# Layer 0's self-attention: the second head's weights turned by VectorE in blocks of 32 and moved by DMA; stacks built with fewer DMA issues

## The chip, the cores and the metric

The kernel runs on one core of a Trainium2 chip. The core has a matrix engine (TensorE, PE), a vector engine (VectorE, DVE), an activation engine (ScalarE, ACT), a general engine (GpSimd, POOL) and a queue engine that mostly issues DMAs (SyncE, SP). Tiles live in SBUF, 128 partitions wide; matmul results land in PSUM, in banks of 128 x 512 float32. The metric is the device time of one launch in microseconds; runs of one kernel are given with their median.

## The reference

A decoder with two layers, six sublayers in all, each with a residual and a layer normalisation behind it. The batch is 2, the sequence 1024, the width 256, in float32. Of the six, the change is in the first:

```python
def _L0_attn_ref(x, w_q, w_k, w_v, w_o):        # 16 heads, d_k 64
    scale = 1.0 / sqrt(64)
    q = einsum('bsd,hdk->bhsk', x, w_q)         # k and v the same with w_k, w_v
    scores = einsum('bhqk,bhmk->bhqm', q, k) * scale
    weights = softmax(scores, axis=-1)
    z = einsum('bhqm,bhmk->bhqk', weights, v)
    z = z.transpose(0, 2, 1, 3).reshape(b, s, h * dk) @ w_o
    return x + z

x = layernorm(x + L0_attn(x))
x = layernorm(x + L0_xattn(x, ctx))             # cross-attention and a small MLP
x = layernorm(x + L0_ffn(x))                    # 8 experts, entmax gates
x = layernorm(x + L1_attn(x))                   # 16 heads of 16
x = layernorm(x + L1_xattn(x, ctx, mask))
x = layernorm(x + L1_ffn(x))                    # quantised
```

So the first sublayer's result is 2x + z, normalised. The gates of the expert layer are an entmax: a power of a half (a square root) is taken once in them.

## The kernel before

`l0_attn` (from L205) works on head pairs: two heads of one batch entry, 16 pairs `u` in all. A pair has eight steps of 128 queries each, so the main loop has 128 steps `n`. Every step handles both heads of its pair, `h` = 0 and 1.

The stages of one pair are these.

- `load(u)` (L225) fetches the pair's `w_q`, `w_k` and `w_v` with six DMAs of 64 KB into a tile of the pool `wqkv`, which has two buffers. It runs 12 steps before the pair's first step.
- `project(u, k, blk)` makes q and k of both heads, 64 rows each, transposed, 512 columns at a time. ACT copies the result out of PSUM into half of a tile of the pool `x`. It runs 9 steps ahead for k and 5 steps ahead for q.
- `split` cuts each of these blocks in two parts that float32r matmuls can multiply well: DVE masks off the low bits (L262, `top`), and POOL subtracts that from the whole (L263, in place, on 128 x 512). Then SP copies the parts into stacks (L278). In the q stack of a head, `top` lies over the rest; the k stacks of a head hold `top` twice and the rest twice. One matmul over 128 rows then adds two of the partial products. A pair needs 16 of these DMAs for k and 8 for q, 128 KB each.
- `values` makes v for the pair, as two halves, 7 and 3 steps ahead.
- `scores(n)` (L311; L304 for the first pair, which isn't split) puts 128 queries against 1024 keys into a `wide` tile of two PSUM banks. There are two such tiles, one for each head.
- `most` (L325, DVE) takes each row's negated maximum, `exponentials` (L330, ACT) the exponential of 128 x 1024 with its row sum, and `normalised` the reciprocal of the sum (L338, DVE) and the multiplication with it (L339, POOL).
- `turn` (L352) transposes the head's 128 x 1024 weights on PE, as eight blocks of 128 x 128 into two banks, and `copy` takes each bank into a tile of the pool `weights` (L70 on DVE, L74 on ACT), one bank each.
- `mix` (L373), every second step, multiplies the turned weights of two steps (256 queries) with v: 16 matmuls, eight for each head.
- `output` (L390, L396, L398) multiplies the gathered heads with `w_o`, after each four pairs, in the odd steps, and adds 2x.

The order of PE, DVE and ACT is written out by hand in the main loop. Step `n` computes the scores and exponentials of step `n + 2` and turns the weights of step `n`:

```python
for n in range(steps):
    scores(n + 2)
    most(n + 2, 0)
    ps = turn(n, 0)
    copy(n, 0, 0, ps, nc.scalar)
    exponentials(n + 2, 0)
    copy(n, 0, 1, ps, nc.vector)
    most(n + 2, 1)
    exponentials(n + 2, 1)
    normalised(n + 2, 0)
    if n % 2 == 0:
        mix(n // 2 - 1)
    else:
        others(n - 1)
        others(n)
    ps = turn(n, 1)
    normalised(n + 2, 1)
    copy(n, 1, 0, ps, nc.vector)
    copy(n, 1, 1, ps, nc.scalar)
    parted(n)
```

`others` holds the loads, projections, values and output projections; they run in the odd steps. `parted` holds the calls of `split`. What POOL and SP do is put in order by the scheduler, within what the data allows.

Three further places are touched. `constants` (L107) loads small inputs during the first steps of the stage. In the expert layer, `entmax` (L715 to L773) is a generator, `gates`, whose six pieces are run as jobs inside the second and third round (`n` = 1 and 2) of the loop that computes the experts; its third `yield` comes right after the power, on POOL (L759), and the next piece begins with DVE's use of it (L761). `prepare` (L1308) makes things ready for the second layer. The pools that matter: `weights` has 5 buffers of 128 x 2048, `x` 6 and `r` 4 of 128 x 1024, `p` (the exponentials) 5 of 128 x 1024.

Of the kernel before, what the change touches and what calls it, by code (L numbers as in the profile page):

```python
# [14 lines left out]
ALU = mybir.AluOpType  # L15
# [17 lines left out]
class Decoder:  # L33
# [73 lines left out]
    def constants(self):  # L107

        nc, t, const = self.nc, self.t, self.const
        rows = const.tile([P, P], F32, name="rows")  # L110
# [18 lines left out]
        self.lbv = row("lbv", t["L1_attn_b_qkv"][2 * D : 3 * D], D)  # L129
        self.lbp = row("lbp", t["L1_attn_b_proj"], D)  # L130
# [6 lines left out]
        ctxn = const.tile([P, D], F32, name="ctxn")  # L137
# [71 lines left out]
    def l0_attn(self):  # L209
# [5 lines left out]
        with ExitStack() as s:  # L215
            pool = lambda n, k: s.enter_context(self.pool(n, k))
            pwp, qkp, vp, pp = pool("wqkv", 2), pool("qk", 2), pool("v", 2), pool("p", 5)
# [20 lines left out]
            def project(u, k, blk):  # L238
                ps = self.bank()
                for c in range(2):  # L240
                    nc.tensor.matmul(
                        ps, lhsT=wqkv[u][:, k, c, :], rhs=xT[2 * (u // NP) + blk][:, c, :],
                        start=c == 0, stop=c == 1,
                    )
                if u == 0:
                    if k == 0:
                        out = qs[0, blk] = qkp.tile([P, 512], F32R, tag="q0", name="q0", bufs=3).bitcast(F32)
                    else:
                        if blk == 0:
                            ks[0] = qkp.tile([P, S], F32R, tag="k00", name="k00").bitcast(F32)  # L250
                        out = ks[0][:, blk * 512 : (blk + 1) * 512]
                    self.evac(out, ps, None if k else 0.125, by=nc.scalar)
                    return
                both = self.xp.tile([P, 4, D], F32, tag="x", name="xg").rearrange(
                    "p (a i) d -> p a (i d)", a=2
                )
                halves[u, k, blk] = both[:, 0, :], both[:, 1, :]
                self.evac(both[:, 0, :], ps, None if k else 0.125, by=nc.scalar)

            def split(u, k, blk):  # L260
                x, top = halves.pop((u, k, blk))
                nc.vector.tensor_scalar(top.bitcast(I32), x.bitcast(I32), -4096, None, ALU.bitwise_and)  # L262
                nc.gpsimd.tensor_tensor(x, x, top, ALU.subtract)  # L263
                cols = slice(blk * 512, (blk + 1) * 512)
                for h in range(2):
                    rows = slice(64 * h, 64 * h + 64)
                    if k == 0:
                        st = qs[u, h, blk] = qkp.tile([P, 512], F32R, tag=f"q{h}", name=f"q{h}", bufs=3)
                        stacks = [(st, (top, x))]
                    else:  # L270
                        if blk == 0:
                            ks[u, h] = [
                                qkp.tile([P, S], F32R, tag=f"k{h}{i}", name=f"k{h}{i}") for i in range(2)
                            ]
                        stacks = [(ks[u, h][i][:, cols], (part, part)) for i, part in enumerate((top, x))]
                    for st, parts in stacks:
                        for i, part in enumerate(parts):
                            nc.sync.dma_start(st[64 * i : 64 * i + 64, :].bitcast(F32), part[rows, :])  # L278
# [15 lines left out]
            def scores(n):  # L294
# [20 lines left out]
                for h in range(2):  # L315
                    prob[n, h] = (
                        sc[h], self.sm.tile([P, 1], F32, tag="nm", name="nm"),
                        self.sm.tile([P, 1], F32, tag="sum", name="sum"),
                        pp.tile([P, S], F32, tag="p", name="p"),
                    )  # L320
# [20 lines left out]
            turned = {}  # L341
# [22 lines left out]
            def mix(m):  # L364
# [5 lines left out]
                for kt in range(8):  # L370
                    for h in range(2):
                        rows = slice(64 * h, 64 * h + 64)
                        nc.tensor.matmul(  # L373
                            av[rows, 0:256], lhsT=vals[u][:, kt, rows], rhs=turned[m, h][:, kt, :],
                            start=kt == 0, stop=kt == 7,
                        )
# [46 lines left out]
            for u in range(B * NP):  # L423
                first = 8 * u
                at(first - 12, load, u)
# [23 lines left out]
            with self.tc.manual_schedule(engines=engines):  # L449
# [14 lines left out]
                begin(1)  # L464
                parted(-1)
                wo = self.weight(t["L0_attn_w_o"].rearrange("(g p) d -> p g d", p=P), NP, D)
                next(constants)
                for n in range(steps):
                    scores(n + 2)
                    most(n + 2, 0)  # L470
                    ps = turn(n, 0)
                    copy(n, 0, 0, ps, nc.scalar)
                    exponentials(n + 2, 0)
                    copy(n, 0, 1, ps, nc.vector)
                    most(n + 2, 1)
                    exponentials(n + 2, 1)
# [6 lines left out]
                    ps = turn(n, 1)  # L483
                    normalised(n + 2, 1)
                    copy(n, 1, 0, ps, nc.vector)
                    copy(n, 1, 1, ps, nc.scalar)
# [319 lines left out]
    def l0_ffn(self):  # L806
        nc, t = self.nc, self.t
        HT = GT // 2
        with ExitStack() as s:
# [157 lines left out]
            with self.tc.manual_schedule(engines=engines):  # L967
                start = [begin(b) for b in range(B)]
                mixed = None
                for n in range(len(steps) + 1):  # L970
# [6 lines left out]
                    if n in (1, 2):  # L977
                        for k in range(3):
                            jobs[4 + 4 * k] = lambda: next(gates)
# [328 lines left out]
    def prepare(self, tmp):  # L1308
        nc, t, late = self.nc, self.t, self.late
        H = 16  # L1310
        mask = tmp.tile([P, T // P, SK], U8, name="mask")
# [442 lines left out]
```

## Time and profile before

| what | us |
|---|---|
| three runs | 2685.15, 2685.04, 2682.86 (median 2685.04) |
| the profiled execution, its own time | 2682.37 |
| its span | 2680.6 |
| of the span, up to 930: layer 0's self-attention | 930 |
| 930 to 1190: cross-attention, and the expert layer's start | 260 |
| 1190 to 1230: the gates' last pieces, beside the experts | 40 |
| 1230 to 1900: the experts, then the second layer's projections and attention | 670 |
| 1900 to the end: the rest of the second layer | 781 |

The busy time of the engines in these stretches, as the stretch table gives it, with the granted clock of PE:

| stretch | PE | DVE | ACT | POOL | PE clock |
|---|---|---|---|---|---|
| 30 to 930 | 893.50 | 561.92 | 473.74 | 368.27 | 1.00 |
| 930 to 1190 | 242.84 | 92.98 | 59.64 | 56.14 | 0.93 |
| 1190 to 1230 | 33.84 | 21.43 | 8.45 | 20.44 | 0.87 |
| 1230 to 1900 | 667.62 | 363.48 | 218.18 | 231.91 | 1.00 |
| 1900 to 2680 | 701.91 | 594.00 | 381.45 | 118.11 | 0.93 |

How to read the lines that follow. A group of instructions is given as line, engine, operation, output from inputs, shapes and count, then its busy time in us and the mean of one instruction in ns, then how long the engine stood idle just before them and what ended most of that. A line of the timeline is: start in us, duration, engine, line, operation, output from inputs, shapes and count, and in brackets the wait before it with its releaser. A line of the stretch table is: the stretch, its length, then for each engine its busy time and count of instructions, then the granted clock of PE, the busy share of the DMA engines and GB/s. "SPq" is SP's queue, where a duration is the time that issuing took.

### The profile page before, as it was taken

What the parts mean: (1) busy time and instruction counts of PE and PEld (TensorE: products, weight loads), DVE (VectorE), ACT (ScalarE), POOL (GpSimd) and SP (SyncE); (2) the same over time, 40 slices, a digit from 0 to 9 for tenths busy, and PEclk for the clock granted to TensorE, in tenths of its full rate; (3) what the DMA queues carried; (4) which work ended last, traced back from release to release, by engine and by line L of the source; (5) the groups of instructions that cost most, each with busy time, mean ns of one, the idle gap of its engine ahead of it and who ended that gap; (6) DMA issues with size and microseconds to landing.
All of it is one profiled execution on the core that took longest, in us unless ns stands there. A gap on an engine that the chain in (4) does not pass through costs nothing. (4 is left out here: it accounts for less than half of the span.)

```text
span 2680.6 us, 41386 instructions
## 1 busy us (share of the span) xinstructions
PE 2562.0 (96%) x16113; PEld 1910.0 (71%) x16113; DVE 1641.2 (61%) x3204; ACT 1151.9 (43%) x1808; POOL 798.1 (30%) x615
## 2 busy tenths in 40 slices
PE   8999999999999999899999999999979999998975
PEld 5777777777777656688999999999954444444652
DVE  4666566666656532245555565554667978895686
ACT  4555455545545522122333333333315655664344
POOL 3344344334444321242333333342311000100421
PEclk9999999999999999998999999999988999999996
DMA  4223223222322020100010010010030321110000
GB/s 123 60 56 83 54 54 70 60 54 64 76 54 50 15 75 16 34 5 17 24 32 17 27 33 32 12 44 5 1 61 3 59 37 32 32 33 1 1 1 32
DMA packets 87906, 102.95 MB, mean 38 GB/s; under 512 B 39496, under 2 KB 57504, under 8 KB 87712
## 3 DMA queue, kind: packets, MB, share of 16 engines
q1 hardware_dynamic: 87200, 99.27, 16.2%
q8 instruction: 128, 2.10, 0.3%
q10 hardware_dynamic: 512, 1.05, 0.2%
q14 instruction: 66, 0.54, 0.1%
HBM read 34.21 MB, written 2.10 MB: 14 GB/s over the span
## 5 line engine op out<-in xcount | busy, mean ns | idle before, releaser
L339 POOL TENSOR_SCALAR p<-p,rs 128x1024 f32<-128x1024 f32 x256 | 287.1, 1122 | 524.2 <-DVE rs L338 524.1
L1126 DVE TENSOR_REDUCE most<-bank 128x1 f32<-128x512 f32 x512 | 325.9, 685 | 55.2 <-PE bank L1120 47.1
L325 DVE TENSOR_REDUCE nm<-wide 128x1 f32<-128x1024 f32 x256 | 311.8, 1219 | 65.2 <-PE wide L311 44.6
L330 ACT ACTIVATE p<-wide,nm 128x1024 f32<-128x1024 f32 x256 | 286.1, 1118 | 96.3 <-DVE rs L338 85.2
L1169 ACT ACTIVATE w<-wide 128x1024 f32<-128x1024 f32 x256 | 248.3, 1022 | 138.1 <-PE wide L1163 129.4
L74 ACT COPY w<-bank 128x512 f32<-128x512 f32 x260 | 152.2, 586 | 321.6 <-PE bank L352 317.2
L352 PEld LDWEIGHTS bank<-ident,p 128*128 128x128 f32 x2048 | 232.6, 141 | 66.8 <-POOL p L339 25.0
L352 PE MATMUL bank<-ident,p 128*128 128x128 f32 x2048 | 270.8, 275 | 3.7 <-ACT w L74 2.2
L311 PE MATMUL wide<-k,q 128*128 128x512 f32 x960 | 252.4, 404 | 3.4 <-ACT p L330 3.4
L70 DVE COPY w<-bank 128x512 f32<-128x512 f32 x260 | 179.1, 689 | 107.7 <-PE bank L352 98.9
L373 PE MATMUL acc<-w,v 128*64 128x256 f32 x2048 | 237.8, 384 | 0.1
L874 ACT ACTIVATE mhT<-mhT,cols 128x256 f32<-128x256 f32 (+1 forms) x256 | 143.2, 607 | 149.9 <-DVE mhT L902 98.9
L373 PEld LDWEIGHTS acc<-w,v 128*64 128x64 f32 x2048 | 143.1, 137 | 76.5 <-issue 12.7
L311 PEld LDWEIGHTS wide<-k,q 128*128 128x128 f32 x960 | 171.2, 189 | 36.5 <-ACT p L330 5.4
L885 PE MATMUL unit<-xT,w 128*128 128x256 f32 x768 | 183.5, 381 | 0.0
L785 POOL TENSOR_TENSOR hs<-hs,mhT 128x1024 f32<-128x1024 f32 x31 | 103.4, 3336 | 262.0 <-DVE hs L783 262.0
L942 DVE SCALAR_TENSOR_TENSOR r<-acc,gates,r 128x128 f32<-128x128 f32 x256 | 77.8, 346 | 140.5 <-PE acc L933 140.5
L1120 PE MATMUL bank<-kst,qst 64*128 64x512 f32 x512 | 149.6, 483 | 12.4 <-DVE most L1126 12.1
L1120 PEld LDWEIGHTS bank<-kst,qst 64*128 64x128 f32 x512 | 70.3, 193 | 121.4 <-DVE most L1126 95.2
L885 PEld LDWEIGHTS unit<-xT,w 128*128 128x128 f32 x768 | 141.3, 191 | 17.2 <-issue 0.7
L181 POOL TENSOR_TENSOR rstd<-ve,nhalf 128x4 f32<-128x4 f32 (+2 forms) x28 | 26.1, 932 | 391.6 <-DVE ve L179 391.2
L1183 PE MATMUL acc<-w,v 128*32 128x512 f32 x1024 | 137.0, 607 | 0.0
(321 smaller groups left out, 4412.1 us busy)
## 6 DMA issues: line engine op xcount, KB each, us to landing
k<-xg SPq DMA_DIRECT2D x240, 128.0 KB, 2.4
w<-in_L_ffn_W SPq DMA_DIRECT2D x16, 1024.0 KB, 5.3
q<-xg SPq DMA_DIRECT2D x120, 128.0 KB, 2.3
qst<-qh SPq DMA_DIRECT2D x60, 64.0 KB, 2.4
qst<-ql SPq DMA_DIRECT2D x60, 64.0 KB, 2.4
kst<-kh SPq DMA_DIRECT2D x60, 64.0 KB, 2.9
kst<-kl SPq DMA_DIRECT2D x60, 64.0 KB, 2.4
xg<-in_x SPq DMA_DIRECT2D x4, 512.0 KB, 4.4
```

Source lines behind the costliest of these rows:

```text
L70: nc.vector.tensor_copy(out, in_)
L74: nc.scalar.copy(out, in_)
L311: nc.tensor.matmul(sc[h][:, kb, :], lhsT=qs[u, h, qt // 4][:, at : at + P], rhs=ks[u, h][i][:, kb * 512 : (kb + 1) * 512], start=i == 0, s ...
L325: nc.vector.tensor_reduce(nm, sc, AX.XY, ALU.max, negate=True)
L330: nc.scalar.activation(p, sc.rearrange("p a c -> p (a c)"), AF.Exp, bias=nm, accum_out=sum_)
L339: nc.gpsimd.tensor_scalar(p, p, rs, 1.0, ALU.mult, ALU.mult)
L352: nc.tensor.transpose(ps[:, k * P : (k + 1) * P], p[:, kt * P : (kt + 1) * P], self.ident)
L373: nc.tensor.matmul(av[rows, 0:256], lhsT=vals[u][:, kt, rows], rhs=turned[m, h][:, kt, :], start=kt == 0, stop=kt == 7,)
L885: nc.tensor.matmul(v[:, m, :], lhsT=up[e][k][:, f : f + P], rhs=self.halves[g][k], start=k in (1, 2, 5) and m == 0, stop=True, skip_group_ ...
L1120: nc.tensor.matmul(sc[a], lhsT=stack[b, jp, "q"][rows, q0 : q0 + P], rhs=stack[b, jp, "k"][rows, kb * 512 : (kb + 1) * 512], start=True, s ...
L1126: nc.vector.tensor_reduce(most[n][:, kb, qt, h : h + 1], sc[a], AX.X, ALU.max, negate=True)
L1169: nc.scalar.activation(slot[:, k, :], ps[k].rearrange("p a q -> p (a q)"), AF.Exp, scale=0.25)
```

## The change

It has five parts.

1. *The second head's weights* are no longer transposed on PE. DVE transposes each 32 x 32 block of the 128 x 1024 tile within its partition quarter (`turn_blocks`), into a tile of a new pool `blocks` that holds two steps. Every second step `move_blocks` brings the blocks into the places that a full transposition gives them: 16 copies of 32 partitions x (8 runs of 64 elements), of which 4 stay in their quarter and are made by POOL, and 12 go to another quarter by DMA, 4 issued by ACT and 8 by SP, 64 KB each. The turned tile has its queries in another order, and `mix` writes the second head's output through a permuted view that puts them back.
2. *The order of a step* changes: DVE's block transposition of step `n + 1` stands between the maxima of the two heads, ACT's moves stand between the exponentials, and the first head's two copies swap their engines. The second head's exponentials now lie in tiles of the pool `r`, and `p` has 3 buffers.
3. *The stacks.* POOL's subtraction is written straight into the stacks, once for each head (64 x 512, eight for each pair in place of four of 128 x 512). `top` of both k blocks lies side by side in one tile, so that the k stacks take four DMAs of 256 KB from `top` and two of 256 KB for the rest, from the half that was written to the other; the q stacks take four of 128 KB.
4. *The weights' buffers:* `wqkv` has one buffer, and `load` runs 11 steps ahead.
5. *Around it:* two of the constants' tiles move into a tile of `r`, two biases of the second layer are loaded in `prepare`, and the six pieces of `gates` run as four jobs of the second round, at the places 4, 7, 10 and 13, and two of the third, at 8 and 12, in place of three each at 4, 8 and 12.

```diff
-            pwp, qkp, vp, pp = pool("wqkv", 2), pool("qk", 2), pool("v", 2), pool("p", 5)
+            pwp, qkp, vp, pp = pool("wqkv", 1), pool("qk", 2), pool("v", 2), pool("p", 3)
+            bp = pool("blocks", 2)
...
             def split(u, k, blk):
-                x, top = halves.pop((u, k, blk))
+                cols = slice(blk * 512, (blk + 1) * 512)
+                x, top = (a[:, cols] for a in halves[u, k])
                 nc.vector.tensor_scalar(top.bitcast(I32), x.bitcast(I32), -4096, None, ALU.bitwise_and)
-                nc.gpsimd.tensor_tensor(x, x, top, ALU.subtract)
...
+                own = [slice(64 * h, 64 * h + 64) for h in range(2)]
+                for h, rows in enumerate(own):
                     if k == 0:
                         st = qs[u, h, blk] = qkp.tile([P, 512], F32R, tag=f"q{h}", name=f"q{h}", bufs=3)
-                        stacks = [(st, (top, x))]
+                        nc.gpsimd.tensor_tensor(st[rows, :], x[rows, :], top[rows, :], ALU.subtract)
+                        nc.sync.dma_start(st[own[1 - h], :].bitcast(F32), top[rows, :])
...
-                    for st, parts in stacks:
-                        for i, part in enumerate(parts):
-                            nc.sync.dma_start(st[64 * i : 64 * i + 64, :].bitcast(F32), part[rows, :])
+                        nc.gpsimd.tensor_tensor(ks[u, h][1][rows, cols], x[rows, :], top[rows, :], ALU.subtract)
+                if k and blk:
+                    for h, rows in enumerate(own):
+                        for half in own:
+                            nc.sync.dma_start(ks[u, h][0][half, :].bitcast(F32), halves[u, k][1][rows, :])
+                    for h, rows in enumerate(own):
+                        st = ks[u, h][1].bitcast(F32)
+                        nc.sync.dma_start(st[own[1 - h], :], st[rows, :])
...
+            def turn_blocks(n):
+                if not 0 <= n < steps:
+                    return
+                m, qt = divmod(n, 2)
+                p = prob.pop((n, 1))[-1]
+                if qt == 0:
+                    blocks[m] = bp.tile([P, 32, 2, 32], F32, tag="blocks", name="blocks")
+                nc.vector.transpose(blocks[m][:, :, qt, :], p.rearrange("p (j q) -> p j q", q=32))
+
+            def move_blocks(n):
+                m, qt = divmod(n, 2)
+                if qt == 0 or not 0 <= n < steps:
+                    return
+                to = turned[m, 1] = self.weight(None, 8, 256)
+                src = blocks.pop(m).rearrange("p (k r) t q -> p k r (t q)", r=4)
+                dst = to.rearrange("p k (i q) -> p k i q", i=4)
+                for d in range(4):
+                    for i in range(4):
+                        r = (i + d) % 4
+                        a, b = src[32 * i : 32 * i + 32, :, r, :], dst[32 * r : 32 * r + 32, :, i, :]
+                        if d == 0:
+                            nc.gpsimd.tensor_copy(b, a)
+                        else:
+                            (nc.scalar if d == 1 else nc.sync).dma_start(b, a)
...
+                        out, p = av[rows, 0:256], turned[m, h][:, kt, :]
+                        if h:
+                            out = out.rearrange("p (t i q) -> p i t q", t=2, i=4)
+                            p = p.rearrange("p (i t q) -> p i t q", t=2, i=4)
...
-                at(first - 12, load, u)
+                at(first - (11 if u else 12), load, u)
...
                 for n in range(steps):
                     scores(n + 2)
                     most(n + 2, 0)
+                    turn_blocks(n + 1)
+                    exponentials(n + 2, 0)
+                    move_blocks(n + 1)
                     ps = turn(n, 0)
-                    copy(n, 0, 0, ps, nc.scalar)
-                    exponentials(n + 2, 0)
-                    copy(n, 0, 1, ps, nc.vector)
+                    copy(n, 0, 0, ps, nc.vector)
                     most(n + 2, 1)
+                    copy(n, 0, 1, ps, nc.scalar)
                     exponentials(n + 2, 1)
                     normalised(n + 2, 0)
                     if n % 2 == 0:
...
-                    ps = turn(n, 1)
                     normalised(n + 2, 1)
-                    copy(n, 1, 0, ps, nc.vector)
-                    copy(n, 1, 1, ps, nc.scalar)
                     parted(n)
...
-                    if n in (1, 2):
-                        for k in range(3):
-                            jobs[4 + 4 * k] = lambda: next(gates)
+                    for k in {1: (4, 7, 10, 13), 2: (8, 12)}.get(n, ()):
+                        jobs[k] = lambda: next(gates)
```

## The prediction

> **What bounds the kernel now.** I read first the page's span and engine table, then the stretch table for one head pair, then the timeline of two steps, then what each queue waited for. A group below means one head pair: eight steps of 128 queries.
>
> ```profile
> span 2680.6 us, 41386 instructions
> PE 2562.0 (96%) x16113; PEld 1910.0 (71%) x16113; DVE 1641.2 (61%) x3204; ACT 1151.9 (43%) x1808; POOL 798.1 (30%) x615
> ```
>
> ```profile
> core 0: us, PE busy (x) PEld busy (x) DVE busy (x) ACT busy (x) POOL busy (x), PEclk, DMA share, GB/s
> 400.00:454.40 54.40, 54.40 (x369) 40.89 (x368) 34.67 (x59) 30.07 (x53) 23.18 (x20) 1.00 0.31 66
> ```
>
> That stretch is one group: weight loads for two successive pairs are issued 54.4 us apart, at 414.47 and 468.85. TensorE (PE) is busy throughout at full clock and every other engine has room. In start-to-start times a group is four steps with `mix` (scores 1.94, first turn 0.96, mix 3.60, second turn 0.86: 7.36), two with projections (1.93, 0.87, 3.43, 0.86: 7.1) and two with values (5.4), 54.4 in all. The two heads turn 16 blocks a step, so half of that is what the change can free.
>
> What would take over is seen where PE has little to do, at the end of the stage:
>
> ```profile
> 893.07 1.20 PE L311 MATMUL wide<-k,q 128*128 128x512 f32 x4 [0.45 <-ACT p L330]
> 893.70 1.11 ACT L330 ACTIVATE p<-wide,nm 128x1024 f32<-128x1024 f32 x1 [0.69 <-DVE rs L338]
> 894.71 0.19 ACT L330 ACTIVATION_READ_ACCUMULATOR p<-wide,nm 128x1 f32 x1
> 895.01 0.17 DVE L338 RECIPROCAL rs<-sum 128x1 f32<-128x1 f32 x1 [1.35 <-POOL p L339]
> 895.09 0.67 DVE L70 COPY w<-bank 128x512 f32<-128x512 f32 x1
> 895.26 1.12 POOL L339 TENSOR_SCALAR p<-p,rs 128x1024 f32<-128x1024 f32 x1 [0.33 <-DVE rs L338]
> 895.67 1.22 DVE L325 TENSOR_REDUCE nm<-wide 128x1 f32<-128x1024 f32 x1
> ```
>
> PE waits here for an exponential. There is a ring: second head's exponential, its reciprocal 1.31 later (895.01 after 893.70), normalisation on POOL, the next maxima, the next exponential. Now it is hidden, because PE takes longer.
>
> **The change, part by part.** *PE:* eight transposes leave each step, 0.86 start to start: 8 x 0.86 = 6.9 a group, 54.4 to 47.5. The permuted output of the second head's mix has runs of 32 elements; at 0, since mix keeps its instruction count, and if each slowed by a tenth it would cost 0.18 a step with mix.
>
> *DVE:* a copy of 0.69 leaves each step and one 32x32-block transpose of 128x1024 enters. No row has it. Below it lies the two-elements-a-cycle row (L262, 444 ns for 512, so at most 0.9), above it two passes at the reduction's rate, 2.4. It is nearest to the reduction of the same 1024 elements at 1.22, 1.14 to the next instruction as rows overlap. DVE goes from 34.7 to about 34.7 - 5.5 + 9.8 = 39, still below PE. What matters is its place: it stands between the two maxima, in order, and waits for POOL's normalisation of the step before.
>
> *The ring, from the start of a second head's exponential:* reciprocal at 1.31, normalisation at 1.56 to 2.68, transpose from 2.78 (the first maximum, 1.22 from 1.39, fits beside it), next instruction 1.14 later at 3.92, copy 0.58, second maximum 1.22, and 0.11 to its exponential (895.67 + 1.22 to the next in such steps): 5.83 a step. That is close to the 47.5 / 8 = 5.94 that PE needs, so the small things decide.
>
> *ACT:* a copy of 0.59 leaves each step; four DMA issues enter every second step, between the two exponentials. The nearest issue has as many pieces of 256 B (64 KB):
>
> ```profile
> 414.47 0.89 SPq L225 DMA_DIRECT2D wqkv<-in_L_attn_w_q  x2
> 415.40 0.97 SPq L225 DMA_DIRECT2D wqkv<-in_L_attn_w_k  x2
> 430.35 10.50 SPq L278 DMA_DIRECT2D k<-xg  x16
> ```
>
> 0.93 for two is 0.47 each (0.37, as the weights of the expert layer, to 0.65, as the stacks, 10.5/16). They can start when the transpose is done, 3.92; 4 x 0.47 brings 5.8, the copy queued behind them 0.49, and the exponential starts at 6.4 in place of 5.83. Behind ACT stands DVE's reciprocal, and behind it POOL. A step with mix is then 6.4, which PE needs too (1.94 + 0.87 + 3.60). A group: 4 x 6.4 + 2 x 6.25 (projection, PE) + 2 x 5.85 = 49.8, and the masking of the top bits (0.38 each, two of them, in front of a maximum in two steps, partly beside a wait) makes it 51.
>
> *POOL* is where I expect the gain to go. Its order, as the scheduler leaves it, is: four subtractions after a projection, four block copies, then the two normalisations of the step.
>
> ```profile
> L339 POOL TENSOR_SCALAR p<-p,rs 128x1024 f32<-128x1024 f32 x256 | 287.1, 1122 | 524.2 <-DVE rs L338 524.1
> L263 POOL TENSOR_TENSOR xg<-xg 128x512 f32<-128x512 f32 x60 | 78.4, 1325 | 29.5 <-DVE xg L262 29.5
> L1036 POOL MEMSET w<- 32x128 f32 x4 | 0.8, 197 | 0.2
> L1041 POOL MEMSET cz<- 128x512 f32 x1 | 0.5, 529 | 0.1
> L1034 POOL MEMSET w<- 128x128 f32 x2 | 0.4, 206 | 14.4 <-PE unit L885 14.4
> ```
>
> The subtractions become twice as many, each on 64 partitions. The memsets on 32 and on 128 partitions take 197 and 206 ns, so fewer partitions save nothing: 1.30 each (0.65, were it halved, to 1.33). A block copy has 512 elements a partition: between the memset's 0.53 and half a normalisation plus its fixed part, 0.66; I take 0.6 (0.3 if partitions did count, 1.33 if it ran as a two-input operation). Between two normalisations of a second head POOL then has 4 x 1.30 + 4 x 0.6 + 2 x 1.12 = 9.8 in a step that lasts 6.4 + 0.75 = 7.15. The transpose of the next step waits 2.7, and behind it on DVE the copy, the second maximum, and so ACT, the scores and PE. Twice a group, of which some half microsecond in all is caught up again: 51 + 5 = 56, 1.6 above now; over 15 groups +24.
>
> *Stretches with output projections* cost 13.8 now in each of three batches (groups of 57.8 and 64.6). Half of these matmuls fall into the odd steps in which PE would now wait: -7 each, -21. The stage: +3.
>
> *SP and DMA:* 24 stack issues a group become 10 larger ones, 32 moves join. A move has two steps, some 12.5 us, to land before its mix. After a projection, SP first waits for the subtractions (5.2), then sends eight moves, 8 x 0.47 = 3.8, with landing 2.4 as the stacks: 11.4 plus the last stacks, 1-2, inside the 15 that remain to that mix (two steps, scores and a turn). Cover is thin; without it PE would wait 1 to 3 once a group. At 0. The other loads are 12 us ahead of use.
>
> *Start:* one weight buffer in place of two. The second pair's loads wait for the first's values (PE, 21.5), four issues 1.9 and landing 2.1 bring 25.5, where that projection now starts at 21.54: +4. Nothing hides it.
>
> *Expert layer:* the power on POOL moves a job earlier and gets its time.
>
> ```profile
> 1196.21 10.54 POOL L759 TENSOR_TENSOR esq<-u,eroot 128x64 f32<-128x64 f32 x1 [1.89 <-DVE u L758]
> 1206.79 0.23 DVE L761 TENSOR_TENSOR esq<-emean,esq 128x64 f32<-128x64 f32 x1 [10.14 <-POOL esq L759]
> ```
>
> PE stood still for 5.95 behind this, then ran 6.7 us at half clock, 3 more: -9 (0 if DVE meets another wait). The moved biases and constants ride on SP ahead of use: 0.
>
> *Clock.* PE would now stand still 2 to 3 us twice a group, and the trace has a price for that:
>
> ```profile
> 26.50:29.90 3.40, 0.85 (x5) 0.29 (x2) 2.52 (x3) 1.55 (x3) 0.06 (x1) 1.00 0.01 1
> 929.90:933.30 3.40, 1.29 (x11) 0.84 (x8) 2.05 (x5) 2.72 (x6) 1.20 (x2) 0.99 0.02 5
> 933.30:936.70 3.40, 3.31 (x16) 2.04 (x18) 1.11 (x2) 0.52 (x2) 1.04 (x1) 0.51 0.00 0
> ```
>
> A wait of 2.5 near 27 kept the clock, one of 2.2 near 931 halved it for 3.4 us, a loss of 1.7, and it would fall on the steps with mix, where PE has nothing to spare. 30 waits x 1.7 = 51 at worst, 0 at best; with one in two, +25.
>
> The page "TensorE: Matmul & The Clock Gate" of the Trainium skill (Part 1: The HAM clock gate) asks for an idle window of about 3.4 us before the clock halves. By that rule waits of 2.7 would cost nothing and the sum would be 25 lower; the row near 931 speaks against it. The skill's "SBUF — State Buffer" (SBUF: two separate sides) lets GpSimd be shut out by DVE only when DVE runs two-port or has two SBUF inputs; were a transpose to count as that, POOL would lose up to 8 x 1.2 a group more, by the rule nothing, and no run shows it yet.
>
> **Sum**, against the profiled execution, 2682.4 (span 2680.6, 1.8 around it): +3 + 4 - 9 + 25 = +23, 2705. The median of the runs, 2685.0, lies 2.7 above that execution: 2708.
>
> **Rivals.** (1) *POOL is in time, so faster.* If subtraction and copy together take under (7.15 - 2.24)/4 = 1.23 in place of 1.9, the transpose never waits. The group is 51, -3.4 x 15 = -51, some 7 a batch of output projections still fits into PE's gaps, -15 with the thin end of it, then +4 and -9, no clock loss: 2614. For it: POOL is idle 58% of a group; against it: the memset rows. If the ring gave nothing at all, PE's 47.5 would set -104, 2576. (2) *The transpose runs two passes* (2.3): the ring grows 1.14 in every step, of which 6.8 a group shows: +105 beside the 5 of POOL, 2790. For it only that no row has it. (3) *A block copy costs 1.1 and more*, as a two-input operation would: 4 x 0.5 twice a group and then in every second step: about +110, 2800. (4) *Moves land late*: PE waits at mix once a group, 15 x 2 = +30, 2740; DMA share 0.31 with room speaks against it.
>
> **How the numbers follow.** Forecast 0.55, rival (1) 0.25, (2) and (3) 0.08 each, (4) 0.04. The forecast's own range is 2683 (no clock loss) to 2735 (all). The range for eight in ten goes down into (1), to 2640, and up to 2785, short of (2). About 0.2%, 5.4 us, is what a measurement here tells from no change: faster 0.32 (all of (1) and a lower end of the forecast), same 0.13, slower 0.55.
>
> **What would show it.** In the profile after: groups of about 56 with PE busy under 90% in them; DVE's transposes near 1.2 and, twice a group, waiting 2 to 3 on POOL's normalisation; block copies 0.5 to 0.7, subtractions near 1.3; ACT's issues about 0.5; the granted clock under 1.00 in the stage; DVE's wait on the power gone. I am wrong if the transposes find POOL done, if PE stays near 100% there, or if mix waits on a DMA.

## The result and the profile after

The changed kernel takes 2757.81 us (median of four runs, 2754.06 to 2764.29), the kernel before 2683.95 beside it: a ratio of 1.0277, 95% interval 1.026 to 1.0295. It is slower, as forecast, but by 74 us where 23 were forecast.

The page of the changed kernel, its span and engine table:

```profile
span 2762.5 us, 39964 instructions
PE 2522.1 (91%) x15086; PEld 1838.2 (67%) x15089; DVE 1712.4 (62%) x3204; ACT 1081.8 (39%) x1680; POOL 1031.3 (37%) x931
```

PE is busy 40 us less, and yet the span is 82 longer. One pair in the stretch table (the wqkv issues that were 54.4 apart are now 59.8 apart, 398.97 and 458.80):

```profile
400.00:460.00 60.00, 50.41 (x304) 35.45 (x304) 39.70 (x58) 25.68 (x45) 38.09 (x40) 0.97 0.47 95
```

PE now stands still for 9.6 of 60 us, and no other engine is near 60. So the bound is a chain across engines, not one engine's work.

To see which chain, I took the start of the second head's exponential in every step, from the timeline of ACT, and its distances. This is worked out from the trace, for one ordinary pair of each kernel, in order of the pair's steps (in the second distance the projection of k ran, in the sixth that of q, in the fourth and eighth the values):

```
                    distances between the second heads' exponentials, us              sum
before   at 420.0   7.35  7.09  7.36  5.38  7.36  7.10  7.35  5.39                    54.4
after    at 409.6   5.71 10.63  5.83  7.42  5.71  8.74  7.72  7.36                    59.1
after, last pair, no projections: 7.20 and 6.4-6.5 in turn                            54.6 for eight
```

Before, the steps are PE's. After, there is a short step of 5.71, the ring as forecast (5.83), and a step of 7.2 to 10.6, in which ACT issues its four moves. Even without any projection the two together are 13.65, as long as before's 54.4 / 4 = 13.6, projections included (before's last pair, without projections, has 7.35 + 5.30 = 12.65). The timeline of the engines in the step of 10.63:

```profile
416.81 1.12 POOL L349 TENSOR_SCALAR r<-r,rs 128x1024 f32<-128x1024 f32 x1 [0.31 <-DVE rs L348]
417.03 1.51 DVE L265 TENSOR_SCALAR xg<-xg 128x512 int32<-128x512 int32 x2 [0.31 <-ACT xg L74]
418.30 5.44 POOL L278 TENSOR_TENSOR k<-xg 64x512 fp32r<-64x512 f32 x4 [0.36 <-DVE xg L265]
420.86 4.41 ACTq L379 DMA_DIRECT2D w<-blocks  x4
422.47 0.13 DVE L348 RECIPROCAL rs<-sum 128x1 f32<-128x1 f32 x1
423.80 2.57 POOL L377 COPY w<-blocks 32x512 f32<-32x512 f32 x4
425.46 0.59 ACT L74 COPY w<-bank 128x512 f32<-128x512 f32 x1 [4.49 <-issue]
425.95 1.12 ACT L340 ACTIVATE r<-wide,nm 128x1024 f32<-128x1024 f32 x1
426.47 1.12 POOL L349 TENSOR_SCALAR p<-p,rs 128x1024 f32<-128x1024 f32 x1
427.19 0.16 DVE L348 RECIPROCAL rs<-sum 128x1 f32<-128x1 f32 x1 [3.99 <-ACT r L340]
427.21 1.19 PE L318 MATMUL wide<-k,q 128*128 128x512 f32 x4 [3.38 <-ACT r L340]
427.56 1.13 POOL L349 TENSOR_SCALAR r<-r,rs 128x1024 f32<-128x1024 f32 x1
```

ACT is in its four issues ("ACTq", which the engine table doesn't count as busy) from 420.86 to 425.3. The copy behind them waited 4.49, the exponential comes at 425.95, DVE's reciprocal and PE's scores wait for that. POOL's burst, four subtractions and four copies, lies beside the issues and ends at 426.4, just in time. Ahead of all this DVE's two masks (L265) take 1.51, and the first maximum (418.47) and the transposition (419.60) stand behind them. The costs of the parts, from the page's groups:

```profile
L363 DVE STREAM_TRANSPOSE blocks<-r 128x1024 f32<-128x1024 f32 x128 | 158.6, 1239 | 30.8 <-POOL r L349 25.0
L377 POOL COPY w<-blocks 32x512 f32<-32x512 f32 x256 | 155.5, 608 | 64.8 <-DVE blocks L363 45.6
```

The subtractions, from the group table of the stage alone, and ACT's issues, from the table of one source line (least, median and greatest duration of one in ns, first and last start):

```profile
L271 POOL TENSOR_TENSOR q<-xg 64x512 fp32r<-64x512 f32 x60 | 78.3, 1305 | 11.5 <-DVE xg L265 8.1
```

```profile
L379 ACTq DMA_DIRECT2D w<-blocks x256: 592/626/1752, 41.3 to 1031.0; - x128
```

Transposition, block copy and subtraction cost what the forecast took (1.24, 0.61, 1.31). The issue does not: 0.626 in place of 0.47, and up to 1.75.

Of the 82 us between the two profiled executions (the changed kernel's is the slowest of its four, 6.5 above their median), 93.2 arise in the stage of the change (its last exponential starts at 1024.85 in place of 931.66), and 11 are won behind it. Within the stage the first eight steps cost 20.2 more (78.8 for 58.6), the last pair 2.2, the fourteen pairs between 70.2 (879.3 for 809.1), 5.0 each; the first exponential is 0.6 later.

### The profile page after: what moved, and what is told of

Same layout as the page of the kernel before. It is cut to its first block, busy times and chain, and to the rows that moved or that the text cites. A ratio compares the mean times of both kernels' runs of the same rounds, so it can differ in the third digit from the quotient of the medians.

```text
span 2762.5 us, 39964 instructions
## 1 busy us (share of the span) xinstructions
PE 2522.1 (91%) x15086; PEld 1838.2 (67%) x15089; DVE 1712.4 (62%) x3204; ACT 1081.8 (39%) x1680; POOL 1031.3 (37%) x931
## 5 line engine op out<-in xcount | busy, mean ns | idle before, releaser
L318 PE MATMUL wide<-k,q 128*128 128x512 f32 x960 | 296.8, 443 | 116.3 <-ACT r L340 86.0
L340 ACT ACTIVATE p<-wide,nm 128x1024 f32<-128x1024 f32 x128 | 142.7, 1115 | 250.3 <-DVE nm L335 196.3
L415 PE MATMUL acc<-w,v 128*64 128x256 f32 x2048 | 236.5, 382 | 0.0
L349 POOL TENSOR_SCALAR p<-p,rs 128x1024 f32<-128x1024 f32 x128 | 143.7, 1123 | 246.3 <-DVE rs L348 240.1
L415 PEld LDWEIGHTS acc<-w,v 128*64 128x64 f32 x2048 | 142.3, 137 | 75.8 <-issue 12.5
L377 POOL COPY w<-blocks 32x512 f32<-32x512 f32 x256 | 155.5, 608 | 64.8 <-DVE blocks L363 45.6
L340 ACT ACTIVATE r<-wide,nm 128x1024 f32<-128x1024 f32 x128 | 143.1, 1118 | 92.5 <-DVE rs L348 92.5
L363 DVE STREAM_TRANSPOSE blocks<-r 128x1024 f32<-128x1024 f32 x128 | 158.6, 1239 | 30.8 <-POOL r L349 25.0
L349 POOL TENSOR_SCALAR r<-r,rs 128x1024 f32<-128x1024 f32 x128 | 143.9, 1125 | 84.4 <-DVE rs L348 84.2
L74 ACT COPY w<-bank 128x512 f32<-128x512 f32 x132 | 76.8, 583 | 228.5 <-DMA w<-blocks 83.3
L390 PEld LDWEIGHTS bank<-ident,p 128*128 128x128 f32 x1024 | 138.0, 157 | 28.6 <-issue 8.8
L390 PE MATMUL bank<-ident,p 128*128 128x128 f32 x1024 | 153.5, 300 | 1.8 <-DVE w L70 1.8
```

Of the source, the lines that this page charges most:

```text
L318: nc.tensor.matmul(sc[h][:, kb, :], lhsT=qs[u, h, qt // 4][:, at : at + P], rhs=ks[u, h][i][:, kb * 512 : (kb + 1) * 512], start=i == 0, s ...
L340: nc.scalar.activation(p, sc.rearrange("p a c -> p (a c)"), AF.Exp, bias=nm, accum_out=sum_)
L349: nc.gpsimd.tensor_scalar(p, p, rs, 1.0, ALU.mult, ALU.mult)
L363: nc.vector.transpose(blocks[m][:, :, qt, :], p.rearrange("p (j q) -> p j q", q=32))
L377: nc.gpsimd.tensor_copy(b, a)
L390: nc.tensor.transpose(ps[:, k * P : (k + 1) * P], p[:, kt * P : (kt + 1) * P], self.ident)
```

## The experiments

The theory at first: ACT's issues in the ring set the loss. The rivals: POOL's burst behind the projections, as forecast; moves that land late; the one weight buffer at the start. All times below are medians; the kernel before ran at 2683.05 to 2684.84 beside them, and the changed kernel at 2757.8. Its own runs lie 10 us apart, so a gain of 6 to 10 from one edit is hardly told from none.

### One limit removed at a time

*All moves on SP.*

```diff
-                            (nc.scalar if d == 1 else nc.sync).dma_start(b, a)
+                            nc.sync.dma_start(b, a)
```

> The changed kernel with all twelve moves of two steps issued by SP; ACT issues none. In the changed kernel's trace ACT's four issues take 2.6 us in plain steps and 4.4 in the step behind the k projection, between the two exponentials. Theory A (ACT's issues alone set the loss): the plain steps with mix go from 7.2 to 5.8-6.4 and the step behind the k projection from 10.7 to about 7.3; a pair falls from 60 to about 52, the kernel to 2620-2660. Theory B (POOL's subtractions and block copies are the bound, the issues lie beside them): the two steps behind a projection stay at 16.5 together, nothing gained, 2740-2760. Mixed (each hides the other: plain steps gain 1, the steps behind projections nothing since POOL's burst takes over): a pair 57.5, the kernel about 2715. Theory C (moves land late): SP has 12 x 0.61 = 7.3 us of issues in two steps beside the stacks, and mix would wait on a DMA: slower than 2757.

Measured: 2742.46, ratio to before 1.0217 (1.0201 to 1.0232). A pair's distances at 710.6 are 8.20 7.31 9.14 6.14 8.22 7.32 9.14 5.71, in all 61.2. The steps with a projection fell from 10.6 to 7.3, as theory A has it, but the steps behind them rose from 5.8 to 9.14: 16.45 for two, as before. Theory A alone is wrong, B alone too, since something was gained; it is the mixed case, with less gained than its 2715. The ordinary pairs did not get shorter at all: the six without output projections and other extras average 61.0 here, 60.1 in the changed kernel and 54.4 before. The gain lies in the first eight steps (70.7 for 78.8) and in pairs with output projections (the longest 65.9 for 72.2).

*One subtraction for a block.*

```diff
+                nc.gpsimd.tensor_tensor(x, x, top, ALU.subtract)
...
-                        nc.gpsimd.tensor_tensor(st[rows, :], x[rows, :], top[rows, :], ALU.subtract)
-                        nc.sync.dma_start(st[own[1 - h], :].bitcast(F32), top[rows, :])
+                        nc.sync.dma_start(st[own[0], :].bitcast(F32), top[rows, :])
+                        nc.sync.dma_start(st[own[1], :].bitcast(F32), x[rows, :])
```

> The changed kernel with POOL's subtraction as before, once on 128x512 in place, so four in a pair in place of eight; the stacks' low halves then take two more DMAs for k and four more for q on SP. ACT's issues stay. Theory A: the issues alone decide, so no gain, 2750-2765. Theory B: POOL has 2.6 us less behind each projection, twice a pair, 15 pairs: up to 78 us less, 2680. Mixed: ACT's 4.4 still stands in the step behind the k projection, so only what POOL adds behind it is gained, some 0.5-1 us a pair, 2740-2755.

Measured: 2748.67 (1.0248, 1.0231 to 1.0266). The step of 10.7 stays, and the time lies within the mixed case's 2740 to 2755.

*Both edits above together.*

> Both edits: all moves on SP, one subtraction per block. Theory A: as the moves on SP alone, 2620-2660. Theory B: as the one subtraction alone, about 2680. Mixed (the two hide each other, so that only both together free the step): clearly better than the sum of the two single gains, a pair about 53, the kernel about 2650. Theory C (SP has 12 moves, and 16 stack issues in a pair): slower than the one subtraction alone.

Measured: 2730.82 (1.0177, 1.0161 to 1.0193), 27 less than the changed kernel, the two single gains being 15 and 9. The 2650 of the mixed case did not come. The distances at 394.4 say why: 8.13 7.30 6.27 5.70 **12.56** 7.31 6.28 5.69. Most steps are short now (7.3, 6.3, 5.7), but a step of 12.56 has come. What PE waited for in the stage (in all, times, longest):

```profile
PE acc L415 <- DMA w<-blocks: 56.7, 23, 3.8
PE wide L318 <- ACT r L340: 38.9, 27, 1.7
```

Now mix (L415) waits for moves: SP, with twelve moves every two steps and six stack issues more in each pair, is late. That is theory C, a third limit behind the other two.

*ACT's moves later.* They are issued by ACT as before, but behind the second exponential.

```diff
                     exponentials(n + 2, 1)
+                    while by_act:
+                        nc.scalar.dma_start(*by_act.pop(0))
                     normalised(n + 2, 0)
```

> The changed kernel with ACT's four moves issued behind the second exponential in place of between the two; nothing else. By the runs so far three limits lie one behind the other: ACT's issues in the ring (2.6 to 4.4 each second step), POOL's burst behind a projection, and SP's queue. Theory (stacked limits): plain steps with mix fall from 7.2 to 5.8-6.4, the steps behind a projection stay near 16.5 for two, as with all moves on SP: 2725-2745. Rival (ACT's issues are the whole loss, and putting all of them on SP was spoilt by SP alone): a pair near 52, 2640.

Measured: 2751.44 (1.0248, 1.0232 to 1.0263). This takes the issues out of the ring without loading SP, and again almost nothing is gained. POOL and DVE in the step behind a projection, in two timelines of this kernel:

```profile
417.99 2.57 POOL L379 COPY w<-blocks 32x512 f32<-32x512 f32 x4
420.67 1.12 POOL L349 TENSOR_SCALAR p<-p,rs 128x1024 f32<-128x1024 f32 x1
421.76 1.12 POOL L349 TENSOR_SCALAR r<-r,rs 128x1024 f32<-128x1024 f32 x1
```

```profile
418.08 0.16 DVE L348 RECIPROCAL rs<-sum 128x1 f32<-128x1 f32 x1 [0.72 <-ACT r L340]
418.16 1.22 DVE L335 TENSOR_REDUCE nm<-wide 128x1 f32<-128x1024 f32 x1
422.91 1.25 DVE L363 STREAM_TRANSPOSE blocks<-r 128x1024 f32<-128x1024 f32 x1 [3.53 <-POOL r L349]
```

The second head's sum is known at 418.08; its normalisation begins at 421.76, because POOL still has block copies and the first head's normalisation. DVE's transposition waits 3.53, and the second maximum behind it. This is the wait of the forecast (2.7), in its place. It appears in full here and with all moves on SP; in the changed kernel ACT's issues lie beside it, and only 8 transpositions wait more than 2. With it comes the clock, in the stretch table of the same kernel:

```profile
422.70:426.10 3.40, 0.60 (x3) 0.16 (x1) 3.19 (x5) 0.14 (x1) 0.26 (x2) 0.92 0.75 117
426.10:429.50 3.40, 2.28 (x6) 1.79 (x7) 2.61 (x4) 1.97 (x3) 2.16 (x2) 0.50 0.11 24
429.50:432.90 3.40, 3.40 (x20) 2.35 (x20) 2.24 (x4) 1.68 (x4) 2.71 (x5) 0.58 0.25 53
```

PE has nothing to do for almost a whole row, and for the following 6.8 us its granted clock is half (0.50, 0.58). Of the two steps behind such a wait the first takes 6.14 and the second mostly 8.2 to 9.0, where both take 6.1 to 6.2 once both limits are removed.

*POOL's order by hand.* Block copies behind the normalisations, and one subtraction a step.

```diff
+            engines |= {mybir.EngineType.Pool}
...
-                            nc.gpsimd.tensor_copy(b, a)
+                            own_quarter.append((b, a))
...
                     normalised(n + 2, 1)
+                    while own_quarter:
+                        nc.gpsimd.tensor_copy(*own_quarter.pop(0))
                     parted(n)
...
-                        nc.gpsimd.tensor_tensor(ks[u, h][1][rows, cols], x[rows, :], top[rows, :], ALU.subtract)
+                        rest = (ks[u, h][1][rows, cols], x[rows, :], top[rows, :], ALU.subtract)
+                        later.setdefault(n + 2 * blk + h, []).append(lambda rest=rest: nc.gpsimd.tensor_tensor(*rest))
```

> The changed kernel with POOL's order written by hand: the block copies behind the two normalisations, and one subtraction a step in place of four at once. The same work; ACT's issues stay between the exponentials. Theory (stacked limits): ACT's issues still hold the steps with mix at 7.2 and more; behind the projections they took 4.4 us and hid most of POOL's burst, so little is gained: 2735-2755. Rival (POOL's burst is the loss, as the forecast had it): 2 x 2.7 a pair, 15 pairs, 81 less and the clock with it: under 2680.

Measured: 2748.25 (1.0238, 1.0212 to 1.0265). DVE's transpositions wait for POOL only 8.2 us in the whole stage (25.0 in the changed kernel), and it helps little: ACT's issues still hold the steps, at 10.5 behind the projection of k and at 7.6 to 9.1 elsewhere.

### Both limits removed

The last two edits together:

> The changed kernel with ACT's moves behind the second exponential and POOL's order by hand, without the early load. Apart these two gave -6 and -10. Theory (each of the two limits hides the other): together they give over 100: pairs of 50.7 as with the early load, the start 10 to 15 later than there: 2630-2645. Rival (what made the three edits fast was the early load): 2735 or more.

Measured: 2624.12 (0.9781, 0.9767 to 0.9796). Alone, ACT's later issues gave 6 and POOL's order 10; together they give 134. Put the other way, with the other limit gone ACT's issues in the ring cost 124 (2748.25) and POOL's order as the scheduler left it 127 (2751.44). A pair at 578.0: 6.11 7.36 5.70 6.18 6.09 7.40 5.70 6.17, in all 50.7. One thing isn't separated here: POOL's order also sends part of k's stacks later, and ACT's issues shortly behind a k stack's issue, 0.93 on average with ACT's moves late alone, take 0.68. With the early load beside them:

> The changed kernel with three edits: ACT's moves behind the second exponential, POOL's order by hand (block copies behind the normalisations, one subtraction a step), and the second pair's weights loaded at once into a tile of the pool ao, which is free then. No work is left out. Theory (stacked limits, each removed): a step near PE's 5.94, or 6.4 with mix, a pair of 48.5-50.5, the start 10-20 less late: 2600-2640, faster than both kernels. Rival (SP's queue is the next limit: 32 moves of 0.65, 21 us, 10 stacks and 6 loads, 9 us, in a pair of 49, and mix waits on them): 2650-2700.

Measured: 2622.45 (0.9763, 0.9748 to 0.9777). One pair in its stretch table:

```profile
401.80:452.60 50.80, 48.84 (x308) 34.03 (x306) 39.57 (x57) 25.45 (x46) 37.65 (x40) 1.00 0.54 112
```

PE works 48.8 of 50.8 at full clock; DVE, ACT and POOL do as much as in the changed kernel. Mix waits for no move there, so SP is off the path. A last edit on top of these writes SP's order by hand too:

```diff
-            engines |= {mybir.EngineType.Pool}
+            engines |= {mybir.EngineType.Pool, mybir.EngineType.SP}
```

> The fastest so far (ACT's moves late, POOL's order by hand, early load) with SP's order by hand too, in the order of the program. In its trace SP waits 100 us for POOL's subtractions with moves queued behind, but mix waits for no move. Theory: SP is off the path there, the same within 5 us, 2617-2627. Rival: the order by hand lets moves land late or earlier: over 2640, or under 2610.

Measured: 2629.44 (0.9799, 0.9783 to 0.9816), 7 more than without, a little outside what the theory gave. Its pairs are the same 50.7; the difference lies in the first eight steps, 70.6 in place of 64.1, where one distance is 15.91. In that step ACT issues its four moves only from 47.59 on, and the exponential behind them starts at 51.82; what held them back is not shown.

### What the start and an issue cost by themselves

*The early load* alone: while the pool `ao` is free, the second pair's weights go into one of its tiles, 12 steps ahead as before.

```diff
-                w = wqkv[u] = pwp.tile([P, 3, 2, P], F32, tag="wqkv", name="wqkv")
+                if u == 1:
+                    w = aop.tile([P, S], F32, tag="aoT", name="aoT")[:, : 6 * P].rearrange(
+                        "p (k c j) -> p k c j", k=3, c=2
+                    )
+                else:
+                    w = pwp.tile([P, 3, 2, P], F32, tag="wqkv", name="wqkv")
+                wqkv[u] = w
```

> The changed kernel with the second pair's weights loaded at once into a free tile, and nothing else. Forecast: the one weight buffer costs 4. In the changed kernel the first eight steps took 78.8 in place of 58.6, of which PE's wait for the load and the half clock behind it are some 6, and ACT's issues and POOL's burst in the first pairs the rest. Theory: 5 to 8 less, 2750-2753. Rival (the whole late start of 20 comes from the load): 2738.

Measured: 2759.32 (1.0282, 1.0267 to 1.0297): nothing is gained. The first distance is 10.84 again (16.07 in the changed kernel), and the first eight steps 73.2 (78.8), but at the end of the stage only 3.8 are left of it in the profiled execution (last exponential at 1021.07), and the medians show none. Both sizes that were expected are wrong. Of the 20.2 by which the start is late, 8.7 go with ACT's issues and POOL's burst (70.1 with both removed and the late load kept) and 6.0 more with the early load (64.1). The 5.5 that stay no run explains.

*No moves at all*, and then ACT's four alone:

```diff
-                to = turned[m, 1] = self.weight(None, 8, 256)
...
+                tile = blocks.pop(m)
+                turned[m, 1] = tile.rearrange("p (k r) t q -> p k (r t q)", r=4)
```

> The changed kernel with all sixteen moves of two steps left out (ACT's, SP's and POOL's copies): mix reads the block-transposed tile as it is, so the second head's weights lie in wrong places. This shows what the transposition, the new order and the subtractions cost without the moves. Theory (stacked limits): POOL's four subtractions (5.2) and two normalisations (2.24) are 7.4 in a step of 7.3, so the burst is gone too; plain pairs near 50, the start still late, 2620-2650. Rival (the ring itself, with DVE's transposition in it, is the bound): 55 and more a pair, over 2690.

> The changed kernel without SP's eight moves and POOL's four copies; ACT's four moves stay, between the exponentials, and go to a tile that nothing reads; mix reads the block-transposed tile as it is, so the second head's weights lie in wrong places. Without any move it took 2633. Theory (a move's issue costs ACT 0.65 by itself, and the exponential waits for it): four issues 2.6, plain steps with mix 7.2 in place of 6.5, pairs of 54-56, 2670-2700. The long issues (1.1 behind the k stacks): should they stay, it is the stacks in flight; should they fall to 0.65, it was SP's moves. Rival (issues cost ACT little without SP's and POOL's share): 2633-2645.

Measured: 2633.25 (0.9807, 0.9792 to 0.9822) without moves, 2717.22 (1.0125, 1.011 to 1.014) with ACT's four. So these 256 issues with their transfers, and nothing of SP's and POOL's share, cost 84 us in the ring, more than expected: a pair is 56.7 at 386.7 (5.71 10.48 5.70 7.69 5.70 8.65 5.70 7.04) and 52.2 without. Their durations, least, median and greatest:

```profile
L383 ACTq DMA_DIRECT2D w<-blocks x256: 592/622/1852, 41.7 to 984.2; - x128
```

The long ones stay although SP moves nothing here. Worked out from the trace: issues within 6 us behind one of a k stack's take 1.09 on average (60 of them), the others 0.63; in the changed kernel 1.10 and 0.65. Long ones lie where the DMA engines are full, as the two stretches around the step of 10.48 show:

```profile
398.00:401.40 3.40, 2.96 (x22) 1.60 (x18) 2.17 (x4) 0.12 (x2) 3.15 (x4) 1.00 1.01 227
401.40:404.80 3.40, 0.60 (x3) 0.52 (x4) 0.62 (x2) 1.69 (x3) 1.05 (x2) 1.00 1.11 213
```

The column before the last is the DMA engines' busy share: 1.01 and 1.11, while ACT issues from 398.63 on. That the stacks in flight make an issue long is thus likely; no run took the stacks away.

### The gates

> The kernel before with the gates' jobs alone moved (four in the second round, two in the third). The forecast's step: PE's wait of 5.95 behind the power goes, and the half clock behind it: 9 us less than before, 2675. Rival: DVE meets another wait for the power, nothing gained, 2684.

Measured: 2675.84, ratio 0.9966 (0.9953 to 0.9979): 9.0 less, as forecast. DVE's use of the power comes late enough that it no longer waits:

```profile
1179.25 10.54 POOL L759 TENSOR_TENSOR esq<-u,eroot 128x64 f32<-128x64 f32 x1 [10.54 <-DVE u L758]
1193.77 0.87 DVE L761 TENSOR_TENSOR esq<-emean,esq 128x64 f32<-128x64 f32 x1
```

## Why the direction was right and the size was not

- *Direction and the ring:* right. PE stops being the bound, and the ring of exponential, reciprocal, normalisation, transposition, copy and maximum takes its place, 5.71 where 5.83 was worked out. But the forecast had the loss come from POOL's burst, and in the changed kernel it comes from ACT's issues.
- *DVE's and POOL's prices:* right (1.24 for 1.22, 0.608 for 0.6, 1.305 for 1.30). Rivals (2) and (3), dearer transpositions or copies, are out. No run shows POOL shut out by DVE: its normalisation takes 1.12 as before.
- *Masking:* mis-sized, "0.38 each". In the changed kernel 20 of the 60 masks took 1.17 to 1.19 us, the others 0.41 to 0.49; in the kernel before 2 of 60 took 1.5. Each of the 20 starts 0.22 to 0.23 into POOL's normalisation of the second head and ends 0.28 behind its end, as in the two lines at 416.81 and 417.03 above. So DVE was held up by POOL, the other way round from what the forecast weighed. The Trainium skill's "SBUF — State Buffer" (SBUF: two separate sides) has this too, for a DVE instruction in a two-port mode: whichever of the two starts first holds the shared port pair for its whole instruction. Which mode the mask runs in no view here tells. The 20 masks lose 15 us in front of a maximum; what of it is on the path no run separates.
- **ACT's issues: the step that failed.** "A step with mix is then 6.4, which PE needs too": by that the issues cost next to nothing, and their price was too low. "0.93 for two is 0.47 each (0.37, as the weights of the expert layer, to 0.65, as the stacks, 10.5/16)". I chose by the size of the pieces, from a load out of HBM; the stacks, which go from SBUF to SBUF as the moves do, were the right row and stood in the bounds. Four issues take 2.61 in the median, in place of 1.88, so the plain step with mix is 7.2 and not 6.4; 3.92 + 2.61 + 0.49 + 0.11 gives 7.13 by the forecast's own chain. Behind the k stacks four take 4.4 and more, 1.1 each, which lies outside the bounds. ACT's issues alone cost 84 us, and 124 beside the other moves.
- *POOL's burst:* it is there, but it didn't set the changed kernel. "The transpose of the next step waits 2.7, ... Twice a group" would be 30 waits, 81 us; in the changed kernel 111 of 128 transpositions find POOL done, 8 wait more than 2, and all waits for POOL are 25.0. That is one of the forecast's own signs of being wrong. The mis-sized issues lie beside the burst: the forecast added the two, in truth the longer of them counts. Where ACT no longer covers it, the burst costs as much as forecast and more: 127 with the clock, where 15 x 5 + 25 = 100 were forecast. With all moves on SP the waits of the transpositions are these:

```profile
DVE blocks L363 <- POOL r L349: 47.0, 21, 3.6
DVE blocks L363 <- DMA w<-blocks: 41.5, 12, 3.6
```

The profile puts 12 of these 33 waits down to a move, but POOL's normalisation ends 0.03 to 0.04 before each of the 33. They add up to 88.5. That this is 2.7 each is chance: 20 of them are 3.5 to 3.6, the others 0.7 to 2.4.
- *Clock:* mis-sized. "with one in two, +25": 58 us of full clock are missing between 26 and 930 in the changed kernel and 75 with ACT's late moves (none before), not all of it on the path. In four kernels (changed, moves on SP, ACT late, ACT's moves alone) every one of the 69 idle times of PE over 3 us in the stage was followed by half clock within 3 us, of the 51 between 1.2 and 2.5 us 19. In four others (one subtraction, alone and with all moves on SP; POOL's order; the early load) it was 45 of 49 over 3 us. So the wait of 2.2 near 931 that halved the clock was no exception, nor was the one of 2.5 near 27 that kept it. The Trainium skill's "TensorE: Matmul & The Clock Gate" (Part 1: The HAM clock gate) gives a free-running window of about 3.4 us, and its length agrees: the low stretches last 3.4 or 6.8 in all twenty cases of the changed kernel between 60 and 930. That the idle time must fill such a window doesn't agree: 19 of the 69 waits were shorter than 3.41, as were all 19 of the 51.
- *Start:* +20 in place of +4. The load's wait was sized nearly right (the first distance is 5.2 longer, and the early load took 6.0 off the start when the limits were gone). That ACT's issues and POOL's burst hold the first pair too, 8.7, was left out; 5.5 stay open.
- *Output projections:* -21 forecast. Two pairs with them cost some 13.7 more than two others before (61.2 + 61.2 against 54.4), and 8 to 9 more now in the first and third batch; in the second, nothing is gained. That is about -10 in all.
- *Moves late, rival (4):* not in the changed kernel, and hardly with all moves on SP (one wait of 0.3); it comes when SP also carries six more stack issues a pair (56.7 us).
- *Rival (1)* said 51 a pair and 2614 if POOL were in time. With POOL in time alone it is 2748; with ACT's issues moved out of the ring as well, the pair is 50.7 and the time 2622 to 2624.

In sum, against the forecast's +23: the pairs cost 42 more than forecast (70 in place of 24 - 21 + 25 = 28), the start 16, the last pair 2, the later first exponential 0.6, the rest of the kernel 2 less. That is 59 more than +23, the +82 of the two profiled executions; the medians differ by 74.

## What to carry to other kernels

When a chain of engines becomes the bound, several delays can lie side by side in it, and each hides the others: taking one away gave 6, 9, 10 or 15 us, the right two together 134. A small gain from an edit is no proof that its target was harmless; look in the new trace at what the chain waits for next. A DMA issue is work of the engine that issues it, here 0.63 us and more, so it belongs behind what others wait for; and work that is not urgent should not stand in a queue ahead of work that is.

## What the hardware showed unexpectedly

- An issue of a 64 KB move within SBUF holds ACT's queue for 0.59 us at the least, and 1.09 on average shortly behind the k stacks, with the DMA engines' share at 1.0 and more in the two stretches shown, whether SP issues moves then or not. None of this is counted in ACT's busy time of 39%.
- DVE's mask of 128 x 512, 0.42 us by itself, took 1.17 to 1.19 in the 20 cases in which POOL's normalisation had begun 0.22 before it: it ended 0.28 behind that one each time. DVE's maxima and transpositions show no such thing (1.20 to 1.23 and 1.22 to 1.25 throughout).
- DVE's transposition of 32 x 32 blocks runs at the rate of its reduction: 1.239 against 1.214 us for 128 x 1024.
- POOL's subtraction on 64 partitions takes as long as on 128: 1.305 and 1.325.
